# Layer 3's normalization coefficients computed a quarter step sooner, and layer 2's edge columns in three GpSimd operations instead of six

## The chip, the cores and the metric

The kernel runs on one core of one Trainium2 chip. The metric is the device time of one execution in microseconds (us), here the median of three runs. PE stands for TensorE's matrix multiplications, PEld for its weight loads, DVE for VectorE, ACT for ScalarE, POOL for GpSimd, SP for SyncE, which issues most of the transfers.

## What is computed

The input is 16 images of 64 channels and 128 x 128 pixels in float32. Four layers follow one another, each of them a residual, `x = x + L(gn(x))`, where `gn` is a group normalization without weights: in each image, each pair of channels is brought to mean 0 and variance 1.

```python
x = x + L0(gn(x))   # gram = xf xf^T / N per image; conv_w @ (gram @ xf)
x = x + L1(gn(x))   # Scharr filters in x and y, |gx| + |gy|
x = x + L2(gn(x))   # a quarter of the channels shifted left, a quarter right; 3x3 conv + bias
x = x + L3(gn(x))   # 3x3 conv, 1x1 conv, batch norm over all images, clip(leaky(y), 0, 255)
```

The batch normalization at the end needs sums over all 16 images, so the last addition can only be done once everything else is.

## The kernel before, in words

An image is worked on in eight tiles of eight rows for each of its two halves (64 channels x 2 halves fill the 128 partitions; for layers 2 and 3 the two row parities do). Three classes hold the stages: `Front` (layers 0 and 1, line 520), `Layer2` (line 736) and `Layer3` (line 884). A fourth, `Gram` (line 458), prepares layer 0's matrix of a later image. Every stage has a method `at(i, q)`, which issues the work of tile `i` in quarter `q` (0 to 3) of a step.

The order of all work is written out by hand, and the engines work through their queues in just that order. The main loop goes over steps, and in each over four quarters; in each quarter it calls `Layer3`, then `Layer2`, then `Front`, then `Gram`, for all images that are under way, and at the end `tick()` (line 256). Within a quarter some pieces stand ahead of the stages ("first of 3", for instance, line 876) or after them ("last of 3", line 879). A new image enters each stage every eight steps; layer 2 runs ten steps behind `Front` and layer 3 ten behind layer 2. So in the same step layer 3 of image b, layer 2 of image b+1 or b+2, and `Front` of a later one share the engines.

A chain of small operations that computes statistics is a Python generator in the list `chains`. Each `tick()` advances each chain by one link, so that one link falls into each quarter. `coefficients` (line 279) is the chain for layers 2 and 3. Its links are: on DVE the sum over the partial statistics `st` into `s`; on PE the product with a constant matrix that averages over a pair of channels; on DVE the copy `me` and the variance `nv`, then a square root `sd` on ACT (both in `rstd`, line 261); and last, on DVE, the reciprocal, a correction of it and the shift. The result `co` (scale and shift) is handed to `put`. The matrices of layer 0 come from a longer chain, `gram_chain` (line 303), which uses `rstd` too.

Layer 2, tile i (line 794). In quarter 0 DVE adds the edge columns (line 804) to the product of the tile before, then makes the layer's result `x3` of that tile from the product and the bias copy `c`, with its sum as one of the partial statistics; then it makes a difference of rows, `d`, and GpSimd's queue issues two transfers that copy it, shifted, to `qd` (`twin`, line 779). In quarter 1 ACT normalizes the next tile in place (line 828), and GpSimd issues six operations on it: four (lines 832 to 837) save its first and last column, scaled, into `edges`, for the two halves of partitions each, and two (lines 840 and 841) set the first or the last column to zero in the shifted channels. In quarter 2 PE makes the products `one` and part of `two`, and ACT squares the result of the tile before (`square`, line 788), for the second partial statistic. In quarter 3 PE makes the rest of `two`. The copy `c` of `one` with the bias by ACT comes first in quarter 3. The tile `one` has a single buffer in PSUM, shared by the layers 2 and 3, so the next product into `one` on PE has to wait for that copy.

After the last tile, at `i == NS` (8), quarter 1, `square` is issued for it and the chain `coefficients` is appended (lines 844 to 846). Its links fall into quarters 1, 2 and 3 of that step and quarter 0 of the next. In quarter 1 of that next step `Layer3.prepare(0)` (line 890) takes `co`, makes from it on DVE two versions for the image's halves, `edge_lower` and `edge_upper`, and normalizes the first tile of layer 3 on ACT, with `edge_lower` first.

The objects `dve`, `act`, `pe`, `pool` and `sp` only record that their operations keep the program's order; as they issue everything through one helper, nearly all lines of the profile carry its number, L73, and the rows are told apart by the names of the tiles.

Of the kernel before, what the change touches and what calls it, by code (L numbers as in the profile page):

```python
# [10 lines left out]
F32 = mybir.dt.float32  # L11
# [97 lines left out]
def tile_kernel(ctx: ExitStack, tc: tile.TileContext, x, cw_h, w2_t, b2, wbin_t, w1_t, b1, gamma, beta, consts, out):  # L109
# [10 lines left out]
    def k(name):  # L120
        return kc[:, AT[name][0]:AT[name][1]]
# [14 lines left out]
    def flat(ap):  # L136
        return ap.rearrange("p j w -> p (j w)")
# [25 lines left out]
    def sv(name, n=1):  # L163
        return small.tile([P, n], F32, tag=name, name=name)
# [24 lines left out]
    xw = wpool.tile([P, W // 2, C + 1, 2], F32, name="xw")  # L189
    pool.memset(xw[:, :, C, :], 1.0)  # L190

    wb = ring.tile([P, (R + 1) * W + 2], F32, tag="v2", name="wb", bufs=3)
    wb = wb[0:C, 0:9 * C].rearrange("p (y x c) -> p y x c", y=3, x=3)
    w1 = ring.tile([P, R + 1, W], F32, tag="v3", name="w1")[0:C, 0, 0:C]

# [540 lines left out]
    class Layer2:  # L736
# [7 lines left out]
        def load(self, i):  # L744


            b = self.b
            N = (R + 1) * W + 2
            t = ring.tile([P, N], F32, tag="v2", name=f"v2_{b}_{i}", bufs=3)
            for c0, c1, shift in ((0, C // 4, 1), (C // 4, C // 2, -1), (C // 2, C, 0)):  # L750
                cut = R * W + 1 - shift
                parts = [(0, i * R, N)] if i + 1 < NS else [(0, i * R, cut), (cut, -R, N)]
                for at, j, end in parts:
                    for s in range(2):

                        first = j * W + at - 1 + shift
                        src = x2_d[b][W + first:W + first + 2 * C * PLANE].rearrange("(c s n) -> s c n", s=2, n=PLANE)
                        sp.dma_start(t[s * C + c0:s * C + c1, at:end], src[s, c0:c1, 0:end - at])
            self.v[i] = t[:, 1:N - 1].rearrange("p (j w) -> p j w", w=W)
            self.whole[i] = t  # L760

        def store(self, i):

# [15 lines left out]
        def twin(self, n):  # L779
# [5 lines left out]
                flat(q[cols(1 - i), n])[:, 1:CP * (W + 2)], flat(d[cols(i), n])[:, 0:CP * (W + 2) - 1]  # L785
            )

        def square(self, i):
            act.activation(
                junk, tiles3[self.b][i].rearrange("p s j w -> p (s j w)"), AF.Square,  # L790
                accum_out=self.st[:, 1, i:i + 1],
            )

        def at(self, i, q):
            b = self.b
            closing = i + 1 == NS
            m = CP - 1 if closing else CP
            if q == 0:
                if 1 <= i:
                    two = self.p.pop(i - 1)[0]  # L800

                    e = self.edges.pop(i - 1).rearrange("p t (m n) -> p t n m", n=2)
                    for side, w in ((0, 0), (1, W - 1)):
                        dve.tensor_add(two[:, :, :, w], two[:, :, :, w], e[:, side])
                    x3 = ring.tile([P, 2, CP, W], F32, tag="x3", name=f"x3_{b}_{i - 1}", bufs=NS + 2)
                    tiles3[b].append(x3)
                    dve.scalar_tensor_tensor(
                        x3.rearrange("p s j w -> p s (j w)"), two.rearrange("p s j w -> p s (j w)"), 1.0,
                        self.c.unsqueeze(1).to_broadcast([P, 2, CP * W]),
                        op0=ALU.mult, op1=ALU.add, accum_out=self.st[:, 0, i - 1:i],  # L810
                    )
                if 0 <= i < NS:
                    difference("d2", 0, self.v[i], m)
                    self.twin(0)
            if q == 1:
                if i == 0:

                    self.wi = stp.tile([P, 2, 3, P], F32, tag="wi", name=f"wi_{b}", bufs=1)
                    for n, base in ((0, w2[:, 2]), (1, wm)):
                        dve.scalar_tensor_tensor(  # L820
                            self.wi[:, n].rearrange("p k o -> p (k o)"), k("I3"), self.co[:, 2:3],
                            base.rearrange("p k o -> p (k o)"), op0=ALU.mult, op1=ALU.add,
                        )
                if -1 <= i < NS - 1:
                    if i == -1:
                        self.co = coefs2.pop(b)
                    t, f = self.v[i + 1], self.whole.pop(i + 1)
                    act.activation(f, f, AF.Identity, bias=self.co[:, 1:2], scale=self.co[:, 0:1])


                    e = stp.tile([P, 2, R], F32, tag="edges", name=f"edges_{b}_{i + 1}", bufs=3)
                    for side, at in ((0, 0), (1, W + 1)):
                        for rows, j in ((lo, 1), (hi, 0)):
                            n = at + j * W
                            pool.tensor_scalar_mul(
                                e[rows, side], f[rows, n:n + (R - 1) * W + 1:W], self.co[rows, 3 + side:4 + side]
                            )
                    self.edges[i + 1] = e

                    pool.tensor_scalar_mul(t[:, :, 0], t[:, :, 0], k("keep0"))  # L840
                    pool.tensor_scalar_mul(t[:, :, W - 1], t[:, :, W - 1], k("keep1"))
                if i + 2 < NS:
                    self.load(i + 2)
                if i == NS:
                    self.square(i - 1)
                    chains.append(coefficients(self.st, lambda co: coefs3.update({b: co})))
            if q == 2:
                if 0 <= i < NS:
                    t = self.v[i]
                    one = ps_one.tile([P, CP, W], F32, tag="one", name=f"one2_{b}_{i}")  # L850
                    two = ps_two.tile([P, 2, CP, W], F32, tag="two", name=f"two2_{b}_{i}")
                    self.p[i] = two, one
                    shared(one, self.wi[:, 0], t, m)
                    if closing:
                        small_product(one[:, m, :], w0, t[:, R, :])

                    both = self.wi[:, 1]
                    own(two[:, 1], 1, TO_SLOTS, w2, "d2", m, both)
                    if closing:

                        p = two[:, 1, m:CP]
                        issue([taps(0, p, [both], [t[:, R:R + 1, :]]), taps(1, p, [both], [t[:, R - 1:R, :]])])
                if 1 <= i < NS:
                    self.square(i - 1)
                if 1 <= i:
                    self.store(i - 1)
            if q == 3:
                if 0 <= i < NS:
                    t = self.v.pop(i)
                    two, one = self.p[i]  # L870
                    both = self.wi[:, 1]
                    own(two[:, 0], 0, TO_SLOTS, w2, "d2", m, both)
                    if closing:
                        p, srcs = two[:, 0, m:CP], [t[:, R - 2:R - 1, :], t[:, R - 1:R, :]]
                        issue([taps(0, p, [w2[:, 0], both], srcs), taps(1, p, [both, w2[:, 1]], srcs)])
            if q == "first of 3" and 0 <= i < NS:
                self.c = ring.tile([P, CP * W], F32, tag="c2", name=f"c2_{b}_{i}", bufs=1)
                act.activation(self.c, flat(self.p[i][1]), AF.Identity, bias=self.co[:, 5:6])
            if q == "last of 3" and -1 <= i < NS - 1:
                difference("d2", 1, self.v[i + 1], CP if i + 2 < NS else CP - 1)  # L880
                self.twin(1)


    class Layer3:
# [5 lines left out]
        def prepare(self, i):  # L890
# [5 lines left out]
                act.activation(dst, src, AF.Identity, bias=co[:, 1:2], scale=co[:, 0:1])  # L896

            if i == 0:
                self.co = coefs3.pop(b)

                self.edge = {}
                for half in ("lower", "upper"):
                    self.edge[half] = sv(f"edge_{half}", 2)
                    dve.tensor_scalar_mul(self.edge[half], self.co, k(half))
                norm(t[:, 0, :], tiles[NS - 1][:, 1, CP - 1, :], self.edge["lower"])
            else:
                norm(t[:, 0, :], tiles[i - 1][:, 1, CP - 1, :], self.co)
# [67 lines left out]
    def run(stage, b, i, q):  # L975
        if 0 <= b < B and stage.first <= i <= stage.last:
            if (stage, b) not in live:
                live[stage, b] = stage(b)
            live[stage, b].at(i, q)
# [42 lines left out]
    for step in range(starts[2][1] - 2, steps):  # L1022
        for q in range(4):
# [7 lines left out]
            for stage, at in starts:  # L1031
                if stage is Front and q in (1, 3):
                    issue_rest()
                for b in range(B):
                    run(stage, b, step - at - NS * b, q)
            if q == 3:
                for b in range(B):
                    run(Layer2, b, step - starts[1][1] - NS * b, "last of 3")
            for b in range(1, B):
                at, n = pace[b]  # L1040
                if n == 1:
# [18 lines left out]
                rest(work, "u", [R + 1, W + 2], 2)  # L1060
                rest(work, "e", [R, W + 2], 1)
            if step == last_one and q == 0:
                rest(ring, "v2", [(R + 1) * W + 2], 3)
                for t in (diffs["d2"], twins["d2"]):
                    slices(t.rearrange("p n j w -> p (n j w)"), 1)
            if step >= last_one and q == 2:
# [88 lines left out]
```

## Time and profile before

| | |
|---|---|
| median of three runs | 2779.61 us (2778.61 to 2780.83) |
| the profiled execution | 2778.27 us, span 2776.5 us |
| PE busy | 2175.3 us (78%), 14804 matmuls |
| DVE busy | 2192.0 us (79%), 3623 instructions |
| ACT busy | 2112.6 us (76%), 3177 instructions |
| POOL busy | 893.2 us (32%), 1350 instructions |
| `edges` on POOL | 512 operations, 703 ns in the mean |
| masking of `v` on POOL | 256 operations, 930 ns in the mean |
| transfers | 685.96 MB, 247 GB/s in the mean |
| mean granted clock of PE | 0.892 |

The span reaches from the first instruction to the last; the time of an execution is a little longer. The page divides the span into 40 slices of 69 us and gives each engine's busy share as a digit, and PE's clock as a digit too. A row of the waits reads: engine and what it was about to do, what ended the wait, the time in total in us, how many times, and the longest. In the timeline an entry in brackets is the idle time of that engine just before the instruction, and what ended it.

### The profile page before, as it was taken

To read this page: it belongs to the slowest core of one execution; us is meant where nothing else is said; L and a number is where in the kernel's file an instruction comes from. 1 tells how busy PE (TensorE), PEld (TensorE's weight loads), DVE (VectorE), ACT (ScalarE), POOL (GpSimd) and SP (SyncE) were. 2 spreads that over 40 slices of the span, in tenths; PEclk is the share of its full clock that TensorE was granted. 3 is DMA by queue.
4 is the path that set the end of the run, shared out by engine and by line. 5 is a ranking of instruction groups with operands and counts; after the bars stand their busy time and mean duration, and the time that the engine had idled before them with its cause. 6 is when DMAs were issued, how large, how long until landed. Compare 5 with 4: busy or idle time off the path is not lost. (4 is left out here: it accounts for less than half of the span.)

```text
span 2776.5 us, 46105 instructions
## 1 busy us (share of the span) xinstructions
PE 2175.3 (78%) x14804; PEld 886.4 (32%) x14804; DVE 2192.0 (79%) x3623; ACT 2112.6 (76%) x3177; POOL 893.2 (32%) x1350
## 2 busy tenths in 40 slices
PE   6578899999999999999999999999999994000000
PEld 4233433434343434343433342333334641000000
DVE  4999999898989898989899999999996435333332
ACT  4766889898989898989898988999997667333332
POOL 2055434343434343434343344444444300000000
PEclk8689999999999999999999999999999997555555
DMA  8799888988888888888888777878877768999999
GB/s 205 201 229 238 211 216 226 231 215 229 218 227 213 229 221 221 216 230 216 230 218 227 206 188 197 217 202 219 215 199 195 213 196 288 420 420 420 420 420 384
DMA packets 693601, 685.96 MB, mean 247 GB/s; under 512 B 60096, under 2 KB 580448, under 8 KB 693360
## 3 DMA queue, kind: packets, MB, share of 16 engines
q1 hardware_dynamic: 668208, 613.83, 75.2%
q0 software_dynamic: 25152, 69.18, 10.2%
q8 instruction: 119, 1.95, 0.3%
q14 instruction: 122, 1.00, 0.1%
HBM read 346.23 MB, written 268.44 MB: 221 GB/s over the span
## 5 line engine op out<-in xcount | busy, mean ns | idle before, releaser
L73 PE MATMUL two<-d,w 128*64 128x508 f32 (+2 forms) x2560 | 846.8, 588 | 0.0
L73 PE MATMUL two<-d,wi 128*64 128x508 f32 (+3 forms) x1536 | 578.0, 579 | 0.0
L73 POOL DMA_DIRECT2D qd<-d x512 | 270.8, 531 | 903.7 <-DVE d L73 287.4
L73 PE MATMUL two<-qd,pk 128*64 128x512 f32 (+1 forms) x1024 | 519.0, 588 | 13.3 <-DMA qd<-d 12.5
L73 POOL TENSOR_SCALAR edges<-v,co 64x8 f32<-64x8 f32 x512 | 359.9, 703 | 307.7 <-ACT v L73 231.4
L73 DVE TENSOR_TENSOR d<-v 128x512 f32<-128x512 f32 (+1 forms) x512 | 345.6, 678 | 87.6 <-issue 55.5
L73 PE MATMUL one<-v,w 128*64 128x508 f32 (+2 forms) x1600 | 378.6, 599 | 34.8 <-ACT c L73 34.8
L73 PEld LDWEIGHTS two<-d,w 128*64 128x64 f32 x2560 | 263.1, 136 | 314.9 <-issue 278.5
L73 PE MATMUL one<-v,wi 128*64 128x508 f32 (+3 forms) x1536 | 358.5, 599 | 3.1 <-issue 2.6
L73 ACT COPY qd<-d 64x512 f32<-64x512 f32 x512 | 315.4, 616 | 20.8 <-DVE d L73 14.5
L73 DVE SCALAR_TENSOR_TENSOR e<-e 128x1032 f32<-128x1032 f32 (+1 forms) x256 | 312.9, 1222 | 0.0
L73 ACT ACTIVATE xh<-po,co 128x128 f32<-128x128 f32 (+1 forms) x480 | 275.2, 621 | 31.4 <-PE po L73 22.7
L73 POOL TENSOR_SCALAR v<-v,kc 128x9 f32<-128x9 f32 x256 | 234.6, 930 | 12.0
L73 DVE SCALAR_TENSOR_TENSOR y<-two,c 128x1024 f32<-128x1024 f32 x128 | 155.9, 1218 | 102.8 <-ACT v L73 65.4
L73 PEld LDWEIGHTS two<-d,wi 128*64 128x64 f32 x1536 | 175.6, 136 | 186.0 <-issue 169.6
L73 ACT ACTIVATE v<-x,co 128x512 f32<-128x512 f32 (+2 forms) x368 | 234.9, 705 | 0.0
L73 ACT ACTIVATE u<-u 128x1024 f32<-128x1024 f32 x128 | 135.3, 1057 | 106.8 <-DVE u L73 106.4
L73 PE MATMUL po<-x,abd 64*64 64x512 f32 (+1 forms) x1024 | 178.5, 643 | 44.0 <-ACT xh L73 41.0
L73 PEld LDWEIGHTS one<-v,w 128*64 128x64 f32 x1600 | 126.0, 139 | 237.9 <-issue 162.7
L73 PEld LDWEIGHTS two<-qd,pk 128*64 128x64 f32 x1024 | 136.3, 136 | 153.9 <-issue 110.6
L73 PEld LDWEIGHTS one<-v,wi 128*64 128x64 f32 x1536 | 108.9, 138 | 224.1 <-issue 209.0
L73 DVE SCALAR_TENSOR_TENSOR u<-xh 128x1170 f32<-128x1170 f32 x128 | 175.6, 1371 | 5.1 <-ACT xh L73 4.2
(165 smaller groups left out, 3333.9 us busy)
## 6 DMA issues: line engine op xcount, KB each, us to landing
x<-in_x SPq DMA_DIRECT2D x256, 256.0 KB, 4.1
x_d<-u SPq DMA_DIRECT2D x512, 128.0 KB, 3.8
y_d<-y SPq DMA_DIRECT2D x512, 128.0 KB, 4.0
x_d<-x SPq DMA_DIRECT2D x496, 128.0 KB, 2.6
xr<-in_x SPq DMA_DIRECT2D x120, 512.0 KB, 6.4
qd<-d POOLq DMA_DIRECT2D x256, 130.0 KB, 3.1
qd<-d POOLq DMA_DIRECT2D x256, 129.8 KB, 3.9
v<-x_d SPq DMA_DIRECT2D x448, 72.1 KB, 3.3
```

Source lines behind the costliest of these rows:

```text
L73: return self.tc.keep_in_program_order(call(*args, **kwargs))
```

## The change

Layer 3's coefficients: the square of layer 2's last tile is issued at the end of quarter 0 of step `i == NS` ("last of 0", after all stages) instead of in quarter 1, and the chain is appended in quarter 0. Its links then fall into quarters 0, 1, 2 and 3 of the same step. A new method `done` receives `co` at the end of the last link and makes `edge_lower` and `edge_upper` there; `Layer3.prepare` only takes them over.

GpSimd: the tile `t` is padded to 10 whole rows of 128, so that a view `by_row` gives its first two elements of every row. These two are the last element of the row before, and the first of this row, in the shifted layout. One `tensor_mul` for each half of the partitions takes both columns of nine rows at once, with the two factors broadcast over the rows; `edges` so has the form rows x 2, and the two additions on DVE read it with a stride. One more `tensor_mul` sets both end columns, with the two masks broadcast. The padding is not loaded or computed on.

```diff
-            t = ring.tile([P, N], F32, tag="v2", name=f"v2_{b}_{i}", bufs=3)
+            t = ring.tile([P, (R + 2) * W], F32, tag="v2", name=f"v2_{b}_{i}", bufs=3)
...
-            self.whole[i] = t
+            self.whole[i] = t[:, 0:N], t.rearrange("p (j w) -> p j w", w=W)
...
+        def done(self, co):
+
+            edge = {}
+            for half in ("lower", "upper"):
+                edge[half] = sv(f"edge_{half}", 2)
+                dve.tensor_scalar_mul(edge[half], co, k(half))
+            coefs3[self.b] = co, edge
...
             if q == 0:
+                if i == NS:
+                    chains.append(coefficients(self.st, self.done))
                 if 1 <= i:
...
-                    e = self.edges.pop(i - 1).rearrange("p t (m n) -> p t n m", n=2)
+                    e = self.edges.pop(i - 1)
                     for side, w in ((0, 0), (1, W - 1)):
-                        dve.tensor_add(two[:, :, :, w], two[:, :, :, w], e[:, side])
+                        dve.tensor_add(
+                            two[:, :, :, w], two[:, :, :, w],
+                            e[:, side:side + R, side].rearrange("p (m n) -> p n m", n=2),
+                        )
...
-                    e = stp.tile([P, 2, R], F32, tag="edges", name=f"edges_{b}_{i + 1}", bufs=3)
-                    for side, at in ((0, 0), (1, W + 1)):
-                        for rows, j in ((lo, 1), (hi, 0)):
-                            n = at + j * W
-                            pool.tensor_scalar_mul(
-                                e[rows, side], f[rows, n:n + (R - 1) * W + 1:W], self.co[rows, 3 + side:4 + side]
-                            )
+                    e = stp.tile([P, R + 1, 2], F32, tag="edges", name=f"edges_{b}_{i + 1}", bufs=3)
+                    for rows, j in ((lo, 1), (hi, 0)):
+                        pool.tensor_mul(
+                            e[rows], by_row[rows, j:j + R + 1, 0:2],
+                            self.co[rows, 3:5].unsqueeze(1).to_broadcast([C, R + 1, 2]),
+                        )
                     self.edges[i + 1] = e
 
-                    pool.tensor_scalar_mul(t[:, :, 0], t[:, :, 0], k("keep0"))
-                    pool.tensor_scalar_mul(t[:, :, W - 1], t[:, :, W - 1], k("keep1"))
+                    ends = t[:, :, 0:W:W - 1]
+                    pool.tensor_mul(
+                        ends, ends, kc[:, AT["keep0"][0]:AT["keep1"][1]].unsqueeze(1).to_broadcast([P, R + 1, 2])
+                    )
                 if i + 2 < NS:
                     self.load(i + 2)
-                if i == NS:
-                    self.square(i - 1)
-                    chains.append(coefficients(self.st, lambda co: coefs3.update({b: co})))
...
+            if q == "last of 0" and i == NS:
+                self.square(i - 1)
...
             if i == 0:
-                self.co = coefs3.pop(b)
-
-                self.edge = {}
-                for half in ("lower", "upper"):
-                    self.edge[half] = sv(f"edge_{half}", 2)
-                    dve.tensor_scalar_mul(self.edge[half], self.co, k(half))
+                self.co, self.edge = coefs3.pop(b)
...
-            if q == 3:
+            if q in (0, 3):
                 for b in range(B):
-                    run(Layer2, b, step - starts[1][1] - NS * b, "last of 3")
+                    run(Layer2, b, step - starts[1][1] - NS * b, f"last of {q}")
```

More of the change, by code (lines that the diff above doesn't have):

```diff
@@ L190, in tile_kernel @@
     pool.memset(xw[:, :, C, :], 1.0)
-    wb = ring.tile([P, (R + 1) * W + 2], F32, tag="v2", name="wb", bufs=3)
+    wb = ring.tile([P, (R + 2) * W], F32, tag="v2", name="wb", bufs=3)
     wb = wb[0:C, 0:9 * C].rearrange("p (y x c) -> p y x c", y=3, x=3)
@@ L826, in at @@
                         self.co = coefs2.pop(b)
-                    t, f = self.v[i + 1], self.whole.pop(i + 1)
+                    t, (f, by_row) = self.v[i + 1], self.whole.pop(i + 1)
                     act.activation(f, f, AF.Identity, bias=self.co[:, 1:2], scale=self.co[:, 0:1])
-                    e = stp.tile([P, 2, R], F32, tag="edges", name=f"edges_{b}_{i + 1}", bufs=3)
-                    for side, at in ((0, 0), (1, W + 1)):
-                        for rows, j in ((lo, 1), (hi, 0)):
-                            n = at + j * W
-                            pool.tensor_scalar_mul(
-                                e[rows, side], f[rows, n:n + (R - 1) * W + 1:W], self.co[rows, 3 + side:4 + side]
-                            )
+                    e = stp.tile([P, R + 1, 2], F32, tag="edges", name=f"edges_{b}_{i + 1}", bufs=3)
[4 more added lines that the diff above has]
+                        )
                     self.edges[i + 1] = e
-                    pool.tensor_scalar_mul(t[:, :, 0], t[:, :, 0], k("keep0"))
-                    pool.tensor_scalar_mul(t[:, :, W - 1], t[:, :, W - 1], k("keep1"))
+                    ends = t[:, :, 0:W:W - 1]
+                    pool.tensor_mul(
+                        ends, ends, kc[:, AT["keep0"][0]:AT["keep1"][1]].unsqueeze(1).to_broadcast([P, R + 1, 2])
+                    )
                 if i + 2 < NS:
                     self.load(i + 2)
-                if i == NS:
-                    self.square(i - 1)
-                    chains.append(coefficients(self.st, lambda co: coefs3.update({b: co})))
             if q == 2:
@@ L1062, in tile_kernel @@
             if step == last_one and q == 0:
-                rest(ring, "v2", [(R + 1) * W + 2], 3)
+                rest(ring, "v2", [(R + 2) * W], 3)
                 for t in (diffs["d2"], twins["d2"]):
```

## The prediction, on record before the changed kernel ran

> **What bounds the kernel now.** I read the page's slices first, then the waits of the whole run, then the timeline around one change of image, and last the busy time in windows of 3.41 us. The slices:
>
> ```profile
> PE   6578899999999999999999999999999994000000
> DVE  4999999898989898989899999999996435333332
> PEclk8689999999999999999999999999999997555555
> ```
>
> From slice 6 on PE and DVE are both near full, and the last sixth is the closing pass, which the change leaves alone. So the question is which of the two carries the time where. In a step without statistics work the timeline has matmuls back to back and one PE step takes 14.85 us (start of the L3 product at 1289.51 to the next at 1304.36); the DVE step takes 14.91. Between two changes of image, at the Gram products of layer 0 (1308 to 1332), DVE idles for PE (4.06 us and 1.31 us before a difference). There the two are brought into step again, and PE is the bound. The waits of the run that touch the change:
>
> ```profile
> ACT sd L73 <- DVE nv L73: 47.6, 54, 3.3
> PE one L73 <- ACT c L73: 34.8, 15, 4.1
> ACT v L73 <- DVE edge_lower L73: 27.0, 15, 3.9
> PE two L73 <- DMA qd<-d: 12.5, 13, 2.6
> DVE d L73 <- POOL v L73: 10.2, 33, 0.9
> ```
>
> The second and third line look like cause and effect. The timeline at 1240 to 1273 (start, us, engine, what; idle before) says otherwise:
>
> ```profile
> 1242.77 1.23 DVE L73 SCALAR_TENSOR_TENSOR x<-two,c 128x1024 f32<-128x1024 f32 x1
> 1242.88 0.68 ACT L73 ACTIVATE c<-one,b_sb 128x512 f32<-128x512 f32 x1
> 1252.23 0.68 ACT L73 ACTIVATE c<-one,co 128x512 f32<-128x512 f32 x1
> 1262.94 0.49 ACT L73 ACTIVATE v<-x,edge_lower 128x128 f32<-128x128 f32 x1 [1.75 <-DVE edge_lower L73]
> 1268.14 0.20 ACT L73 ACTIVATE sd<-nv 128x1 f32<-128x1 f32 x1 [2.05 <-DVE nv L73]
> 1272.92 4.48 PE L73 MATMUL one<-v,w 128*64 128x512 f32 x12 [2.57 <-ACT c L73]
> ```
>
> ACT reaches the bias copy c (1272.18, which frees PSUM for PE) only after a square root of the Gram chain at 1268.14, and that waits for DVE. DVE has no gap at all from 1240 to 1284. If the 1.75 us for edge_lower go, ACT just waits 3.8 us at the square root. DVE's place in its queue decides when PE starts again. And PE pays twice, in the clock (columns: length, PE busy, clock):
>
> ```profile
> 44.80:48.21 3.41, 1.73 (x8) 1.00 0.62 163
> 48.21:51.63 3.42, 1.08 (x4) 1.00 0.60 144
> ...
> 194.99:198.40 3.41, 1.65 (x18) 1.00 1.02 282
> 198.40:201.81 3.41, 3.41 (x10) 0.50 1.05 308
> ...
> 1270.19:1273.60 3.41, 0.84 (x6) 1.00 0.85 233
> 1273.60:1277.01 3.41, 3.41 (x10) 0.50 0.48 106
> ```
>
> A window with 1.65 us busy is followed by one at half clock, one with 1.73 isn't. The product at 1272.92 is followed by the next group at 1277.22, 4.30 us later; 12 matmuls in pairs at 0.427 take 2.56. The gate costs 1.74 us. It strikes so at the seven changes of image from 716.2 to 1535.9 and at 1672.5, eight in all, which are 136.6 us apart.
>
> **What the Trainium skill says.** "TensorE: Matmul & The Clock Gate", section "What's actually happening": PE's clock is halved after an idle window of about 3.4 us, and the windows run freely, whatever the kernel does. The trace agrees: clock 0.50, windows of 3.41. "SBUF — State Buffer", section "SBUF: two separate sides": GpSimd and a DVE instruction with two SBUF inputs exclude each other for a whole instruction. The trace agrees: the same 64x8 GpSimd operation takes 0.30 us at the least and 0.703 in the mean. "GPSIMD Engine Reference", section 3.1: two inputs cost about 2.6 cycles an element; with its 1.2 GHz an estimate for 18 elements is 0.04 us. No run here shows that operation yet.
>
> **The change part by part**, on the boundary at 1240 to 1277; times after are the times shown, moved.
>
> *Square of the last tile a quarter earlier.* It issues one ACT operation and its accumulator read, no DMA; SP keeps its order. It now stands ahead of c at 1242.88 and needs x3, which DVE ends at 1244.00. ACT waits 1.05 and works 1.05, so c comes at 1245.07. Queued behind it are c and four layer 3 norms; PE needs c for its product at 1245.34 and gets it at 1245.81: +0.47.
>
> *Sum of the statistics a quarter earlier.* On DVE it waits for the square's accumulator (1245.20) where DVE would go on at 1244.53: 0.67 lost, and the two wi and all sobel stand behind it. This cannot be below nothing, since x3, square and sum are one chain.
>
> *First half of the coefficients (3 DVE operations, one ACT square root) a quarter earlier.* DVE now reaches nv after u, ending 1254.72. ACT is free at 1252.98 and waits 1.77 at the square root, ahead of c: c at 1254.86 instead of 1252.23. PE, due at 1254.02, starts at 1255.60: +2.20. This is a new stall of 1.58.
>
> *Second half (5 operations) and the two edge operations, from 1261.65 to 1262.94 into the quarter before.* 1.29 us of DVE work, moved and not removed. Before it DVE is 0.67 late, during it 1.98, after it 0.69. The layer 2 difference of 1261.05 is 1.98 later, and so is its GpSimd copy qd, whose second half would land at about 1270.3 instead of 1268.3; PE arrives 2.20 later, so that wait is no worse. The wait of 1.75 for edge_lower goes; what is late next is the square root at 1268.14, now 1268.83. c follows at 1272.87, PE at 1273.61: +0.69.
>
> *So PE.* The idle time at 1266.8 to 1272.9 (1.59 and 2.57 here, 3.9 in one piece at most other boundaries) shrinks to 3.9 - 2.20 + 0.69 = 2.4, and starts again 0.69 later. If no window holds more than 1.7 of it, the halved clock goes: 0.69 - 1.74 = -1.05. If one does, +0.69. The free windows are 3.41 long: a gap of 2.4 in one piece escapes on about 30% of the phases. Now forty windows are 136.53 us. An escaped period is 136.62 - 1.05 = 135.57, so the gap comes earlier in its window each time; a struck one is 137.31, so it comes later. Both push to the edge between striking and escaping, and the mean is held at 136.53: 0.09 less than now, 8 x 0.09 = -0.7.
>
> *GpSimd: 6 operations to 3.* Now 4 x 0.703 + 2 x 0.930 = 4.67 us a tile. The new one isn't in the trace: from 0.30 (shortest of its kind) to 1.8 (longest v operation), three of them 0.9 to 5.4. I take 0.9 each, 2.7, since the wait for DVE's lock, not the work, is what fills these durations. That ends them 2 us sooner, and the 10.2 us that DVE waits for them (0.93 at the most) vanish. Up to 330 us, DVE carries the time and waits 4.6; two waits of DVE for PE there (5.3) swallow some, so two thirds count: -3.0 (from -4.6 to 0; at 1.8 each no wait goes). From 330 to 1672 PE is the bound and hides the waits: 0; without that cover they would be worth the rest, 10.2 - 4.6 - 1.0 = 4.6. From 1672 to 2041 DVE is idle only 2.1 to 2.6 us an image (its busy time against 124.1, 122.3 and 122.4) and is the bound: 1.0 of these waits go, -1.0. DVE's two edge additions (0.170 each) read with a stride of two elements now; counted at nothing, as 8 elements are. The longer v2 tile moves no more data.
>
> *The other boundaries.* 309.6: DVE-bound, +0.7. 447.3: no halved clock, idle 2.3, +0.7. 581.0: idle 2.8, one halved window (587.5) that goes, -1.0. 1796.6 and 1918.9: DVE-bound, 0.7 each, +1.4. From 2041 on DVE and ACT idle 18 us or more an image, which hides it: 0 (0.7 each without that cover).
>
> Sum: -3.0 - 1.0 + 0.7 + 0.7 - 1.0 - 0.7 + 1.4 = -2.9. The profiled execution took 2778.27 (span 2776.5 and 1.8 around it), so 2775.4; it lies 1.3 under the median 2779.61, against which the forecast is 2776.7.
>
> **The rivals.** *The clock is never halved again:* the new stall of 1.58 is just under what trips the gate; a little longer and the half clock falls there, where the 2.4 behind it swallow it, or qd splits the later gap, as at 1268.42. Then 8 x -1.05 = -8.4 instead of -0.7: 2769.0. *It is always halved:* for it, 70% of the phases; against it, that a struck period drifts. 8 x 0.69 = +5.5: 2782.9. *Slower:* the DVE time lost at the sum is paid at all 16 boundaries with the clock halved as now, and GpSimd's new operations, waiting for the lock just as long, give nothing: 16 x 0.69 = +11.0, 2790.6. It decides as soon as the idle time in one window stays over 1.7 at every boundary and a GpSimd operation takes some 1.5 us. For it: DVE has no gap to take the 0.67.
>
> **How the numbers follow.** Held at the edge 0.40, never halved 0.25, always halved 0.17, slower 0.18. Measured runs agree to about 0.2%, 5.6 us, so faster is below 2774.0 and slower above 2785.2. Faster: 0.25 and a little of the first, 0.28. Slower: 0.18 and the late end of the third (GpSimd gains nothing, +4), 0.22. Same: 0.50. The range takes in the first three with GpSimd's bounds: 2769.0 - 2 = 2767 and 2782.9 + 4 = 2787.
>
> **What would show it.** The wait for edge_lower gone and the one at sd larger (about 2.7 a boundary); a new wait of ACT for x ahead of the square and of DVE for the square (0.7); PE waiting twice at c, about 1.6 and 2.4; halved windows at some, not all, of the eight boundaries; boundaries 135.6 or 137.3 apart; no wait of DVE for POOL v. If PE's wait at the second c is gone, DVE is not the chain I take it for, and the gain is larger.

## The result

| | median | runs |
|---|---|---|
| kernel before | 2779.11 us | 2777.71 to 2780.83 |
| changed kernel | 2820.11 us | 2819.35 to 2822.48 |
| ratio | 1.0149 | 95% interval 1.0131 to 1.0166 |

The change costs 41 us. The forecast was 2776.7 with a range up to 2787: wrong in sign and far outside. The slices of the page after, as those shown of before:

```profile
PE   6578899989898989898989899999999995000000
DVE  5999899898989898989898989999997435333332
PEclk8689899999999999999999999999999998555555
```

PE has lost its row of nines: from the ninth slice to the 23rd every second one now has an 8. Two slices are 141 us, about the time of an image, so something is lost once per image. GpSimd did get less to do (538.7 us busy, 893.2 before). The waits of the whole run, in the same form as before:

```profile
ACT sd L73 <- DVE nv L73: 108.5, 51, 6.6
...
PE bank L73 <- DVE av L73: 57.2, 11, 6.3
...
DVE me L73 <- PE bank L73: 41.7, 11, 5.1
...
PE one L73 <- ACT c L73: 26.5, 19, 2.1
...
ACT junk L73 <- DVE x L73: 16.9, 11, 3.0
...
DVE s L73 <- ACT junk L73: 11.7, 16, 1.3
```

The rows for `edge_lower` and for POOL `v`, which the forecast said would go, are gone. The two last rows are the waits that it foresaw (1.05 and 0.67 us a boundary; a single one, below, is 1.13 and 0.68). The second and the third row it did not have: PE waits for the DVE copy `av` 57.2 us (6.5 before), and DVE waits 41.7 us for PE at the copy `me` (none before). One boundary in the timeline of the changed kernel:

```profile
1269.43 1.06 ACT L73 ACTIVATE junk<-x 128x1024 bf16<-128x1024 f32 x1 [1.13 <-DVE x L73]
...
1270.62 0.17 DVE L73 TENSOR_REDUCE s<-st 128x2 f32<-128x16 f32 x1 [0.68 <-ACT junk L73]
...
1276.53 0.15 DVE L73 COPY av<-bank 128x3 f32<-128x3 f32 x1
...
1276.73 0.38 PE L73 MATMUL bank<-s,kc 128*64 128x2 f32 x4 [6.21 <-DVE av L73]
...
1277.06 4.27 PE L73 MATMUL one<-v,wi 128*64 128x512 f32 x12
...
1282.86 0.24 PE L73 MATMUL bank<-kc,pp 128*64 128x1 f32 x4
...
1283.13 0.16 DVE L73 COPY me<-bank 128x2 f32<-128x2 f32 x1 [3.51 <-PE bank L73]
...
1283.77 0.20 ACT L73 ACTIVATE sd<-nv 128x1 f32<-128x1 f32 x1 [5.25 <-DVE nv L73]
1283.88 0.67 ACT L73 ACTIVATE c<-one,co 128x512 f32<-128x512 f32 x1
```

The sum `s` is ready at 1270.8, but the product that needs nothing but `s` and a constant starts at 1276.73, behind `av`. `av` is no operand of it. It reads other columns of the PSUM tile `bank`, into which all small products go, and the product waits for it all the same: uses of that tile keep the order in which they were recorded, whatever their columns (experiments 3 and 4 show it). (The Trainium skill, "PSUM — Partial Sum Buffer", section "PSUM bank collisions raise a hardware error", says to guard PSUM by bank and quarter of the partitions, not by address; so columns alone would be no ground to drop the wait. No run here does without the wait, or gives the coefficients a tile in a bank of its own.) `av` belongs to the Gram chain of a later image; its link is recorded ahead of the product in the same tick, and DVE comes to it only at the end of its quarter. All large products stand behind the waiting one on PE, as the skill's same page says of matmuls ("Engine vs sequencer instructions": they start and complete in program order), and the trace agrees: `one<-v,wi` starts at 1277.06, right behind it.

So PE is 6 us late. A quarter later that comes back to DVE: `me` is recorded behind the Gram chain's next product `bank<-kc,pp`, again on the same tile, and waits 3.51 us for it; ACT waits 5.25 us at `sd`. And the clock, in windows of 3.41 us as in the forecast (length, then the busy times of PE, PEld, DVE, ACT and POOL; the last three columns are clock, DMA share, GB/s):

```profile
1269.79:1273.20 3.41, 0.73 (x8) 0.00 (x0) 2.73 (x6) 3.41 (x8) 1.03 (x2) 1.00 0.99 253
1273.20:1276.62 3.42, 0.00 (x0) 0.00 (x0) 3.42 (x6) 2.51 (x4) 1.98 (x2) 0.51 0.93 266
1276.62:1280.03 3.41, 3.30 (x12) 1.41 (x14) 3.00 (x5) 1.90 (x3) 0.43 (x2) 0.50 0.79 241
```

Two windows are halved, but PE is idle in the first, so the halved clock costs about what it cost before (the 12 matmuls behind it take 4.27 us here and 4.48 there). The loss is the idle time: 6.21 and 1.63 or 1.82 us a boundary, 8.0, against 0.7 and 3.9, 4.6, before. The difference of 3.4 is the growth of the periods, from 136.6 to 140.0.

Where the 42 us of the two profiled spans lie, counted from layer 3's first result of an image (`y` on DVE, whose place in the program no kernel here moves):

| span up to / between these marks, us | before | changed | difference |
|---|---|---|---|
| start to the first mark | 330.4 | 333.3 | +2.9 |
| ten images (a Gram chain at nine of the boundaries) | 1363.2 | 1399.7 | +36.5 |
| three images | 367.3 | 367.5 | +0.2 |
| two images | 208.1 | 209.2 | +1.1 |
| the rest | 507.4 | 508.9 | +1.5 |

Nearly all of it lies in the ten images, and there at the nine boundaries at which a Gram chain uses `bank` in the same quarter. At the first boundary of the ten none does; the product (second line) waits only for `s`, and the period grows by 1.4. The +2.9 at the start hide a tenth such wait (first line): PE waits 7.10 us for `g`, another result that the Gram chain takes from `bank`. The GpSimd part gains at the start (experiment 1), so without it the start loses more, 4.7 (experiment 2).

```profile
296.59 0.38 PE L73 MATMUL bank<-s,kc 128*64 128x2 f32 x4 [7.10 <-DVE g L73]
...
434.72 0.28 PE L73 MATMUL bank<-s,kc 128*64 128x2 f32 x4 [0.16 <-DVE s L73]
```

### The profile page after: what moved, and what is told of

Read it like the earlier page. It is cut to its first block, busy times and chain, and to the rows that moved or that the text cites. A ratio compares the mean times of both kernels' runs of the same rounds, so it can differ in the third digit from the quotient of the medians.

```text
span 2818.7 us, 45754 instructions
## 1 busy us (share of the span) xinstructions
PE 2178.3 (77%) x14804; PEld 896.9 (32%) x14804; DVE 2192.3 (78%) x3623; ACT 2112.3 (75%) x3177; POOL 538.7 (19%) x966
## 5 line engine op out<-in xcount | busy, mean ns | idle before, releaser
L73 PE MATMUL one<-v,w 128*64 128x508 f32 (+2 forms) x1600 | 366.0, 580 | 26.5 <-ACT c L73 26.5
L73 PE MATMUL one<-v,wi 128*64 128x508 f32 (+3 forms) x1536 | 378.8, 628 | 1.8 <-issue 1.4
L73 POOL TENSOR_TENSOR edges<-v,co 64x18 f32<-64x18 f32 x256 | 186.0, 727 | 278.7 <-ACT v L73 240.2
L73 ACT ACTIVATE v<-v,co 128x1154 f32<-128x1154 f32 x128 | 172.0, 1344 | 1.3 <-DMA v<-x_d 1.3
```

What stands on the lines that cost most here:

```text
L73: return self.tc.keep_in_program_order(call(*args, **kwargs))
```

## The experiments

The median of the kernel before was 2778.1 to 2779.2 us beside these runs. "Ten images" means the second row of the table above.

**1. The GpSimd part alone.** The diff of the edge columns, with square, chain and edge scalings of layer 3 where they were before.

> Only the edge columns in three GpSimd operations; the coefficients of layer 3 where they were. Theory A (the coefficients part causes the whole loss): the startup waits of DVE for GpSimd go, as in the changed kernel, about -3 us at the first boundary and little elsewhere: about 2776, range 2772 to 2780, with the ten periods at 136.6 us as before. Rival B (the three wider GpSimd operations hold DVE's memory lock longer and cause the loss): about 2815 to 2820, with periods of about 140.

2778.35 us, ratio 1.0002 (0.9994 to 1.001). Theory A: this part loses nothing. It gains nothing either, though each stage moves: -2.2 at the start, -1.7 in the three images, but +2.9 in the ten and +1.4 in the rest (whose cause was not looked for). The ten lose it at the clock. Before, at the boundary of 447, PE's idle time was cut in two (first fence), and neither piece halved the clock; with GpSimd sooner the transfer of `qd` is no longer late and the idle time is one piece (second fence), with half clock behind it (12 matmuls take 4.10 us, not 2.78):

```profile
452.88 0.61 PE L73 MATMUL two<-qd,pk 128*64 128x512 f32 x1 [1.15 <-DMA qd<-d]
...
455.96 2.78 PE L73 MATMUL one<-v,w 128*64 128x512 f32 x12 [1.15 <-ACT c L73]
```

```profile
453.50 4.10 PE L73 MATMUL one<-v,w 128*64 128x512 f32 x12 [2.52 <-ACT c L73]
```

At 581 the idle time becomes one piece of 2.49 us in the same way. The two periods behind these boundaries grow by 1.7 and 1.4.

**2. The coefficients part alone.** The rest of the diff, with six GpSimd operations as before.

> Only the coefficients of layer 3 a quarter sooner; six GpSimd operations as before. Theory A: 2820 to 2825 us, PE waiting about 6 us at the product bank<-s for DVE av at ten images, periods near 140 us, and up to 5 us more than the changed kernel since the startup waits for GpSimd stay. Rival B (GpSimd's operations are the loss): about 2779.

2820.01 us, ratio 1.0153 (1.014 to 1.0167), ten images at 1399.4. Theory A. The whole loss lies in this part.

**3. The coefficients' link first.** The changed kernel with

```diff
-                    chains.append(coefficients(self.st, self.done))
+                    chains.insert(0, coefficients(self.st, self.done))
```

so that in each tick the link of `coefficients` comes ahead of the Gram chain's. Nothing else is different.

> The changed kernel, with the coefficients' link put ahead of the Gram chain's link in each quarter, so that the product bank<-s is recorded ahead of the DVE copy av<-bank and the copy me<-bank ahead of the Gram chain's product bank<-kc,pp; square, sum and all else stay a quarter early. Theory A (the loss is the wait of two small products on each other's use of the one PSUM tile bank): both waits go (57.2 and 41.7 us in the changed kernel), and the time comes back to about 2777, 2769 to 2783. Rival B (the loss is ACT's and DVE's waiting at the earlier square, sum and square root): stays near 2820.

2781.69 us, ratio 1.0011 (1.0004 to 1.0017). Theory A: one changed call gives back 38 of the 41 us, with square, sum and square root as early as ever. PE's waits at this boundary:

```profile
1243.44 0.28 PE L73 MATMUL bank<-s,kc 128*64 128x2 f32 x4 [0.29 <-DVE s L73]
...
1249.13 0.15 DVE L73 COPY av<-bank 128x3 f32<-128x3 f32 x1
...
1252.13 0.15 DVE L73 COPY me<-bank 128x2 f32<-128x2 f32 x1
...
1252.34 0.38 PE L73 MATMUL bank<-kc,pp 128*64 128x1 f32 x4 [3.71 <-DVE me L73]
```

The product runs as soon as `s` is there, six us ahead of `av`. But the order of the tile now strikes the other way: the Gram chain's product waits 3.71 us for `me`. That is about the size of the 3.9 us that PE waited for `c` before, and mostly replaces it.

**4. An idle product.** The kernel before, with one small product more, whose result nothing reads:

```diff
+    def idle_product():
+        small_product(sm(2), k("gmean"), kc[:, AT["keep0"][0]:AT["keep1"][1]])
+        yield
...
+                    chains.append(idle_product())
```

> The kernel before, with one more small product into the PSUM tile bank, recorded behind the copy av<-bank in the quarter in which the changed kernel has bank<-s; nothing reads it, and its operands are constants, so it waits for nothing but av. Theory A: PE waits about 5 to 6 us for av at that product at ten images, with half clock behind it; part of that replaces the 3.9 us that PE waited later for c, so slower by 5 to 25 us (2784 to 2804). Rival B (the place of a small product on PE costs nothing): within 2 us of 2779.

2804.35 us, ratio 1.0096 (1.0081 to 1.0112), ten images +22.0. Theory A, a little over its upper end: the start loses 5.0 more, where the product waits 6.48 us for `g`. Four tiny matmuls of 0.38 us together, on constants, cost 26 us because of where they stand:

```profile
1268.35 0.38 PE L73 MATMUL bank<-kc 128*64 128x2 f32 x4 [5.29 <-DVE av L73]
```

**5. The Gram chain's product a quarter later**, on top of experiment 3:

```diff
         if b > 1:
             yield
+            yield
         pk = sm(1)
```

> The kernel of the third experiment, with the Gram chain's product bank<-kc,pp and the links behind it a quarter later, so that it no longer shares a quarter with the copy me<-bank. Theory A (the 3.71 us that PE waited there for me were only the order of uses of the tile bank): that wait goes; PE runs on and waits for the bias copy c, about 1.6 us at the first and 2.4 at the second, the two stalls of the forecast; 2770 to 2782, with periods of 136.5 (held at 40 windows of the clock) or, if the halved window goes, 135.6. Rival B (PE has to wait for something at this place whatever the order): a wait of 3 us or more on PE at another instruction, and 2780 to 2790.

2775.99 us, ratio 0.9989 (0.9982 to 0.9995). The wait for `me` is 1.15 us, not gone; the wait for `c` behind it 0.97. Theory A in the time, with the stalls in other pieces than it said. The period of 135.57 is there at six boundaries (135.5 to 135.6), but a halved window that is gone is not what makes it: some of the six have one. PE's idle time in these six periods lies between 3.2 and 5.1 us, DVE's stays at 9.3, which points to DVE's queue as what sets the period.

**6. Product first, `me` last.** The changed kernel, with the coefficients' link ahead of the Gram chain's up to quarter 1, and behind it from quarter 2 on:

```diff
-                    chains.append(coefficients(self.st, self.done))
+                    moved[0] = coefficients(self.st, self.done)
+                    chains.insert(0, moved[0])
...
             tick()
+            if q == 1 and moved[0] in chains:
+                chains.remove(moved[0])
+                chains.append(moved[0])
```

> The changed kernel, with the coefficients' product ahead of the Gram chain's link in its quarter, but the copy me<-bank behind the Gram chain's product in the next: of the two waits only the second is left, DVE at me for PE bank<-kc,pp. Theory A (PE's wait for av is the larger part of the loss, with the half clock that it brings): DVE waits 1 us or less at me since PE is no longer 6 us late, and the time is 2775 to 2790. Rival B (the wait at me carries the loss): DVE still waits 3 us or more, and the time stays over 2805.

2782.36 us, ratio 1.0011 (1.0004 to 1.0017). Theory A: `me` is still ordered behind `bank<-kc,pp`, and does not wait:

```profile
1250.52 0.15 DVE L73 COPY av<-bank 128x3 f32<-128x3 f32 x1
1250.72 0.28 PE L73 MATMUL bank<-kc,pp 128*64 128x1 f32 x4 [0.71 <-DVE av L73]
...
1253.52 0.15 DVE L73 COPY me<-bank 128x2 f32<-128x2 f32 x1
...
1254.15 0.20 ACT L73 ACTIVATE sd<-nv 128x1 f32<-128x1 f32 x1 [1.64 <-DVE nv L73]
1254.26 0.67 ACT L73 ACTIVATE c<-one,co 128x512 f32<-128x512 f32 x1
...
1254.98 2.78 PE L73 MATMUL one<-v,w 128*64 128x512 f32 x12 [1.36 <-ACT c L73]
```

So the 41.7 us at `me` in the changed kernel are a consequence of PE's being late, and the first wait is the cause. This run is also the one closest to the kernel that the forecast had in mind, and its steps are read from it below.

**7. Only square and sum early.** The changed kernel with one more `yield` between sum and product of layer 3.

> The changed kernel, with only the square and the sum a quarter sooner: product, me and all behind it come in the same quarters as in the kernel before. Theory A (square and sum cost ACT 1.05 and DVE 0.67 us of waiting, which the clock's hold at 40 windows swallows): within 4 us of the kernel before, 2774 to 2782. Rival B (the 0.67 us of DVE are paid at each of 16 boundaries): about 2789.

2788.76 us, ratio 1.0038 (1.0024 to 1.0051). Theory A falls. The total is rival B's, but not its parts: the start takes 4.6 less, and ten images take 10.0 more, 1.0 each where B had 0.67. ACT comes to `c` later, PE waits 1.00 us for it at `one<-v,wi`, and the idle time of about 4 us further on stays in one piece and halves the clock at eight of the ten boundaries. The periods are 137.3 in the mean.

**8. Early for eleven images only**, on top of experiment 5: `b < 11` as the condition of the new place, the old code for the last five.

> The kernel of the fifth experiment, with the coefficients a quarter sooner only for the first eleven images; for the last five square, sum, coefficients and edge operations stand where they did in the kernel before. Theory A (in the last images the square ahead of the bias copy c delays PE, which the forecast had at nothing): the stretch from the eleventh boundary to the end gives back the 7.6 us that the fifth experiment loses there, against the first one, so about 2768.5, 2766 to 2772. Rival B (the loss at the end comes from the order of the chains and stays): about 2776.

2773.68 us, ratio 0.9982 (0.9974 to 0.999). Neither number came: a gain of 2 to 3 us on experiment 5, not 7.6 and not 0. The 7.6 was my error: I had counted stages from the operation `edge_lower`, which the change itself moves a quarter ahead. From the neutral mark experiment 5 loses only 2.7 there against experiment 1, and 2.5 came back (365.8, 208.3 and 508.8 against 367.9, 208.9 and 508.6). In the ten images three boundaries have a halved window and the others none, and all but the first two periods are 135.5 to 135.7.

**9. The Gram chain's product later, nothing early**: experiment 1 with the one `yield` of experiment 5.

> The kernel of the first experiment (coefficients as before the change, three GpSimd operations), with the Gram chain's product bank<-kc,pp a quarter later as in the fifth. Theory A (the fifth's periods of 135.57 come from the coefficients being early, which breaks the idle time of 3.9 us at one c into pieces that do not halve the clock): no gain, 2776 to 2782, periods 136.6. Rival B (the gain of the fifth is only that of the Gram chain's place, 0.71 us of wait a boundary): 2768 to 2774.

2769.04 us, ratio 0.9963 (0.995 to 0.9975). Rival B in the time, but not for its reason. This beats both kernels, by 9 us against the one before, and it holds none of the early coefficients. With `bank<-kc,pp` a quarter later the 0.7 us for `av` go, but at the same place PE now waits 0.79 us for `s` (second line). What is shorter is the wait for `c`: 2.7 us or less, not 3.9. The Gram chain's later links moved too, and its second square root, for which ACT waited 2.05 us ahead of several other operations and `c` (1268.14 in the forecast's lines), now stands behind those operations and waits 0.34 (fourth line). That this is the whole gain was not tested by itself.

```profile
1246.02 0.16 DVE L73 TENSOR_REDUCE s<-st 128x2 f32<-128x16 f32 x1
1246.23 0.28 PE L73 MATMUL bank<-s,kc 128*64 128x2 f32 x4 [0.79 <-DVE s L73]
...
1248.96 0.23 PE L73 MATMUL bank<-kc,pp 128*64 128x1 f32 x4
...
1266.68 0.20 ACT L73 ACTIVATE sd<-nv 128x1 f32<-128x1 f32 x1 [0.34 <-DVE nv L73]
1266.79 0.67 ACT L73 ACTIVATE c<-one,co 128x512 f32<-128x512 f32 x1
```

Its undisturbed periods are 134.9 where experiments 5 and 8 have 135.55. DVE's idle time in such a period is 8.7 here and 9.3 in experiment 8, and the wait that is added there is that of `s` for the square, 0.67 us. So with the trouble at `bank` mostly gone (1.15 us or less of waiting for `me` is left in experiment 8), the early coefficients seem to cost the 0.67 us that the forecast gave them.

## Why the prediction was wrong, step by step

*The step that failed* is the one from "Sum of the statistics a quarter earlier" to "First half of the coefficients (3 DVE operations, one ACT square root) a quarter earlier". Between them the chain has a link on PE, the averaging product. The forecast moved it silently and gave it no place, no wait and no price. Its new place decides everything: PE waits 6.2 us at nine boundaries and 7.1 at a tenth. This is shown by experiments 3 and 6 (the link's order alone takes the loss away) and 4 (a product at that place alone makes one).

It could have been foreseen. In the kernel before, both small products stand behind `av` already:

```profile
1245.34 2.80 PE L73 MATMUL one<-v,wi 128*64 128x512 f32 x12
...
1250.15 0.28 DVE L73 TENSOR_TENSOR pp<-bank,ad 128x128 f32<-128x128 f32 x1
1250.35 0.15 DVE L73 COPY av<-bank 128x3 f32<-128x3 f32 x1
1250.42 0.15 DVE L73 TENSOR_REDUCE s<-st 128x2 f32<-128x16 f32 x1
1250.55 0.28 PE L73 MATMUL bank<-kc,pp 128*64 128x1 f32 x4 [0.70 <-DVE av L73]
1250.69 0.26 PE L73 MATMUL bank<-s,kc 128*64 128x2 f32 x4
```

These lines alone do not show the order of the tile: `pp` and `s`, which the two products do read, are done within 0.1 us of `av`. But they show where `av` lies, and the program has its link ahead of the product in the list. A quarter earlier the product comes ahead of `one<-v,wi`, where PE is at 1245.34; `av` is done at 1250.5. If the order holds, that is a wait of over 5 us (an estimate from these two times; experiment 4 measured 5.29), on the engine that the forecast itself called the bound.

*The other steps*, mostly from experiment 6:

| step | forecast | measured |
|---|---|---|
| ACT waits for x3 at the square | 1.05 | 1.13 |
| DVE waits at the sum | 0.67 | 0.68 (0.67 in exp. 6) |
| ACT at the first `sd` | 1.77 | 1.64 |
| PE at the first `c` | 1.58 | 1.36 |
| ACT at the second `sd` (`edge_lower` wait gone) | about 2.7 | 2.75 |
| PE at the second `c` | 2.4 | 2.1 to 2.7 where in one piece |
| halved windows at some of the boundaries | 135.57 or 137.31 apart | 3 of 10; 135.9 to 136.3, or 137.2 apart (the first 138.4) |
| mean period | 136.53 | 136.53 over the ten, 136.3 without the first |
| GpSimd's three operations | 2.7 | 1.87 (2 x 0.727 + 0.416) |
| start; images 1672 to 2041 by GpSimd alone | -3.0; -1.0 | -2.2; -1.7 (exp. 1) |

So the forecast's picture of DVE and ACT held to some tenths. That the mean period agrees to the last digit is luck, since it needs the first period, which the forecast's eight do not hold. Three terms were off even there. GpSimd was put at -4 and gave 0: "from 330 to 1672 PE is the bound and hides the waits: 0" left out that a transfer that is no longer late joins two idle times of PE into one that halves the clock (experiment 1). Experiment 6 came to 2780.2 in its profiled execution, 4.8 over the forecast's 2775.4: 2.1 more in the ten images instead of 1.0 less, and 1.9 more after the last of the three images, where the forecast had nothing. The 2.1 are 3.5 more in the first three periods, where the forecast had -0.3 for the boundaries 447.3 and 581.0, and 1.4 less in the other seven. At 581.0 it counted on -1.0 from the halved window of 587.5; but the period behind that window took 135.2 already, against 136.6 with half clock elsewhere, so it had cost nothing that could be won. Of the 1.9, 0.7 lie in the two images, where experiment 2 has +1.0, so they come with the coefficients, and 1.2 in the rest, where experiment 1 has +1.4, so they come with the GpSimd part; the causes were not looked for. As to the small operations of GpSimd, one of 64 x 18 took 0.23 us at the least, not the 0.04 that the forecast estimated for its work.

The mechanism by which the mean should be held at 40 windows is not shown. The mean is there in experiment 3 (136.51), but in experiment 6 only with the first period, and in experiment 8 periods with and without a halved window were alike.

The rival "slower" named the loss of 0.67 us with the clock halved as now, 2790.6. Experiment 7 comes nearest to it, at 2788.8, but with a gain at the start that this rival ruled out and more than 0.69 a boundary; that the totals lie so close is in part luck. In the changed kernel it is not what happened.

## What to carry to other kernels

When a chain of small steps is moved, walk it link by link and give each link its place in the queue of its own engine: here a product of 0.4 us in front of the bound engine's queue cost what it waited for, 6.2 us. For a tile that several chains share, list every reader and writer in recorded order; here the wait was for the last one ahead, whether or not it had to do with the data. And where idle time sits just at what halves the clock, do not count a removed wait as a gain before looking at which other idle time it joins.

## What the runs showed that I had not expected

The changed kernel's ten periods, 140.0 in the mean, are 41 windows of 3.413 us (139.9), and nearly each of them has two halved windows, 6.8 us, of which PE is idle in one: at these boundaries a stop of 6.2 us cost no more clock than one of 3.9 before. In experiment 9 a period with a halved window is mostly only 0.7 us longer than one without (135.6 and 134.9), though twelve matmuls at half clock lose some 1.3 us (4.10 against 2.78). DVE, near its own bound there, probably hides the rest; that is argued, not shown.

Nor is the limit at which a window halves the clock as sharp as the forecast read it, between 1.65 and 1.73 us of busy PE. In experiment 9 a window with only 1.5 is followed by full clock (columns: length, PE busy, clock, DMA share, GB/s; the ends of matmuls are modelled, so the busy times are rough):

```profile
1263.99:1267.41 3.42, 1.51 (x8) 1.00 0.76 200
1267.41:1270.82 3.41, 3.31 (x16) 1.00 0.96 239
```
